# Moving the router's rows and the product for v on the Vector queue of an attention and MoE kernel

## The chip, the cores and the metric

One core of one Trainium2 chip runs the whole kernel in one launch. The metric is the device time of that launch in microseconds (us), lower is better; a run counts with its slowest core, which is the only one here. PE is the matrix engine (TensorE), DVE the vector engine, ACT the scalar engine, POOL is GpSimd and SP the engine that issues most of the DMAs.

## The reference, cut to what matters

One layer: attention with a layernorm in front of it and a residual, then a mixture of experts with the same. q, k and v come from the same normalised row by a phase and a table of sine and cosine; there are no projections.

```python
x = L0_attn_x                                   # 8 x 1024 x 512, f32
x = x + attn(layernorm(x))
x = x + ffn(layernorm(x))

def attn(x):                                    # 16 heads of 32
    theta_q = xh / (1 + abs(w_q)) + b_q + t * phi_q      # t: the position; k likewise
    Q = concat([cos(theta_q), sin(theta_q)]);  K = ...   # interpolated in a table
    theta_v = xh / (1 + abs(w_v)) + b_v;       V = cos_v + sin_v
    out = softmax(causal(Q @ K.T / sqrt(64))) @ V
    theta_o = out / (1 + abs(w_out)) + b_out
    return cos_o + sin_o

def ffn(x):                                     # 8 experts, 2 of them per token
    probs = softmax(x @ Wr + br)
    gate, expert = top_k(probs, 2)
    pos = place of the token among those of its expert, in order; kept if pos < 160
    y = (relu(rows of an expert @ W1 + b1)) @ W2 + b2
    return sum over the two of gate * y, where kept

def layernorm(x): return (x - mean) / sqrt(var + 1e-5)
```

## The kernel before, in words

**Two stages.** The attention runs as a loop over 32 chunks `n` (L1217): 8 sequences `b` of 1024 tokens by 4 chunks `c` of 128 features (4 heads). Then the experts run, expert by expert (`experts`, L1150). The last router works inside the first expert's time (`ending`, L1362); the other seven work inside the attention loop.

**What a chunk does.** `qk_pre(n)` (L477) turns the normalised rows on PE (transposes, L200, into a PSUM tile) and forms the phases of q and k with four DVE instructions (L493), which read that PSUM tile. `angle` (L423, its instruction L424) makes a second form of them on DVE; ACT computes squares, sines and cosines; `qk_post` (L523) multiplies on DVE and sends q and k to pairs of heads by DMA. `v_pre` (L543: L550, L555, L424) and `v_post` (L563, by `times`, L434) do the same for v without PE. `scores` (L599) multiplies q and k on PE (L608, the causal mask added at L622) and lets ACT take the exponential (L628). `attend` (L634) multiplies that by v on PE (L642) and copies the result out on DVE (L650). `turn` (L666), `o_pre` and `o_post` make the attention's output and its residual for the chunk before.

**PSUM.** `two_banks()` (L193) hands out tiles of a pool of three. Scores, the transposes of `qk_pre`, `turn` and the router, and the router's small products all take their tile from it, so each waits until an earlier user's reader is done.

**The router.** `router(b - 1)` (L695) is a generator that begins at the end of chunk 0 of sequence b (L1327) and is moved on by `next` or by `route_on(slot)`, which does so in chunk `slot` of a sequence. Its parts:
- Statistics, then `inverse_root` (L331), 1/sqrt by an integer guess and Newton steps of three DVE instructions each (L343 to L345). The first layernorm calls it too: 23 calls in all.
- `rows(t)` (L714) normalises 128 tokens on DVE (L716) into one of two buffers `xn2` and issues a store of them for the experts (L722, by SP). Rows 0 and 1 come with the first step.
- `features(g)` (L727), g from 0 to 3, transposes two such tiles on PE (L741) and copies them out on DVE (L743); then, up to g = 2, it makes the next two rows.
- `sums(g)` (L767) multiplies the features by the router's weights on PE (L779), copies the product `lg` (L784), and adds up the one before on PE and DVE (L762, L786).
- Softmax, choice of experts and places follow in chunks 2 and 3.

**What sets the order.** PE, DVE, ACT and SP run in the order in which the program issues its instructions (`manual_schedule`, L121). So an instruction's place in an engine's queue is its place in this program. Around chunk 1 of a sequence, where the router works, the order is, line by line:
- End of chunk 0: the router's statistics, roots and rows 0, 1 (L1327, L1328); v's product for the next chunk (L1344); part of the attention.
- Chunk 1: three steps of attention (L1254); features 0 and rows 2, 3 (L1255); `qk_pre(n + 1)` and `angle` (L1263, L1264); the load of a q/k base on SP (L1267); five scores with v's input between them (L1268); sums 0, then features 1 and rows 4, 5 (L1270, L1271); more attention; sums 1 (L1278); five scores; `turn`, `o_pre` (L1285); features 2 and rows 6, 7, with the store of the sequence's residual rows (L1287); attention; sums 2 (L1314); scores; `qk_pre(n + 2)` (L1330); features 3 (L1334); v's product (L1344); attention; sums 3 (L1346); five scores.

Of the kernel before, what the change touches and what calls it, by code (L numbers as in the profile page):

```python
# [25 lines left out]
NTT = S // P  # L26
# [47 lines left out]
def preln_attn_moe_kernel(  # L74
# [256 lines left out]
    def inverse_root(var, name):  # L331

        n = var.shape[1]
        v = small.tile([P, n], F32, name=f"{name}_v")
        y = small.tile([P, n], F32, name=name)
        t = small.tile([P, n], F32, name=f"{name}_t")
        nc.vector.tensor_scalar(v, var, EPS, None, ALU.add)
        nc.vector.tensor_scalar(
            y.bitcast(I32), v.bitcast(I32), -0.5, ROOT_GUESS, ALU.mult, ALU.add
        )  # L340
        nc.vector.tensor_scalar(v, v, -0.5, None, ALU.mult)
        for _ in range(4):
            nc.vector.tensor_tensor(t, y, y, ALU.mult)  # L343
            nc.vector.tensor_tensor(t, t, v, ALU.mult)
            nc.vector.scalar_tensor_tensor(y, t, 1.5, y, ALU.add, ALU.mult)  # L345
        return y
# [76 lines left out]
    def angle(p, r):  # L423
        nc.vector.tensor_scalar(r, p, TURN_SHIFT, None, ALU.logical_shift_left)  # L424
# [138 lines left out]
    def v_post(n, st):  # L563
        times(v_tiles[n % 2][:, :, :, :DH], heads(st[0]), heads(st[1].bitcast(F32)))


    def o_pre(n, pos):
        c = n % NCH
        p = pos.bitcast(I32)
        r = trig.tile([P, S], I32, name="t_r")  # L570
        nc.vector.tensor_tensor(by_token(p), by_token(pos), along(bias_o, c), ALU.add)
        angle(p, r)
        return p, r
# [86 lines left out]
    def rest(gen):  # L660
        got = None
        for got in gen:
            pass
        return got
# [30 lines left out]
    def router(b):  # L695
# [3 lines left out]
        def store():  # L699
            nc.sync.dma_start(token_tiles(out[b * S : (b + 1) * S, :]), xt)  # L700
# [13 lines left out]
        def rows(t):  # L714
            xn = row2.tile([P, D], F32, name="xn2")
            nc.vector.tensor_scalar(  # L716
                xn, xt[:, t, :], mv[:, t, 0:1], rstd[:, t : t + 1], ALU.subtract, ALU.mult
            )
            for d, (b0, b1_) in zip(xn2_d, REACH):
                if b0 <= b < b1_:  # L720
                    r0 = (b - b0) * S + t * P
                    nc.sync.dma_start(d[r0 : r0 + P, :], xn)  # L722
            return xn
# [3 lines left out]
        def features(g):  # L727

            xT = row2.tile([P, NCH, 2 * P], F32, name="xT", bufs=1)
            if last:  # L730
                for i, xn in enumerate(ahead):
                    ps = pools["ps_tr"].tile([P, NCH, P], F32, name="ps_t")
                    for c in range(NCH):
                        nc.tensor.transpose(ps[:, c, :], xn[:, c * P : (c + 1) * P], ident)
                    copy(xT[:, :, i * P : (i + 1) * P], ps)
            else:
                ps = two_banks()
                for i, xn in enumerate(ahead):
                    for c in range(NCH):
                        at = (NCH * i + c) * 64  # L740
                        by_halves(ps[:, :, at : at + 64], xn[:, c * P : (c + 1) * P])  # L741
                for a in range(2):
                    copy(  # L743
                        xT.rearrange("p c (i a q) -> p i c a q", a=2, q=64)[:, :, :, a, :],
                        ps[:, a, :].rearrange("p (i c q) -> p i c q", i=2, q=64),
                    )
            if g + 1 < NTT // 2:
                ahead[:] = [rows(2 * g + 2), rows(2 * g + 3)]
                if not last and 2 * g + 4 == NTT:
                    store()  # L750
            return xT

        def one_bank():
            if last:
# [39 lines left out]
        lg = None  # L794
        for g in range(NTT // 2):
            xT = features(g)
            yield
            lg = sums(g, xT, lg)
            yield
# [413 lines left out]
    last = None  # L1213
# [3 lines left out]
    for n in range(NCK):  # L1217
        more, late = n + 1 < NCK, last is not None
        b, c = divmod(n, NCH)
        if n == NCK - 1:  # L1220
            to_inputs.close()
            first_rows = experts_begin()
        pos_n = trig.tile([P, S], F32, name="o_p")
        if late:
            e11, halves1, pos = last
        es, halves = [[], []], [[], []]

        products = [attend(n, 0, h, es[h], halves[0]) for h in range(2)]  # L1230
        if late:
            products.insert(0, attend(n - 1, 1, 1, e11, halves1))
        ahead = [scores(pairs[0], h, es[h]) for h in range(2)]
        v_box = [None]
        asides = [keep(v_box, v_pre(n + 1))] if more else [first_rows]
        if b == 0 and c in (1, 2):
            asides.append(layernorm1(1, c - 1))
        elif c == 0 and b + 1 < B:
            asides.append(layernorm1(b + 1, 1))
        elif c == 3 and b + 2 < B:  # L1240
            asides.append(layernorm1(b + 2, 0))
        def route_on(slot):
            if c == slot and route is not None:
                next(route)

        def with_asides(count):
            for _ in range(count):
                some(1, *ahead)
                for g in asides:
                    next(g, None)  # L1250


        if late:
            some(3, *products)  # L1254
        route_on(1)  # L1255
        route_on(2)
        if c == 2 and route is not None:
            asides.append(part(route))
        if n == 0:
            with_asides(2)  # L1260
        if n == 0 or begin:

            qk_st = rest(qk_pre(n + 1))  # L1263
            angle(*qk_st)  # L1264
            angles = keep(place, both(qk_st))
            if begin:
                load_base(n + 2)  # L1267
        with_asides(3 if n == 0 else 5)  # L1268
        rest(residual)
        route_on(1)  # L1270
        route_on(1)  # L1271
        rest(angles)
        if more:
            v_st = v_box[0]
            square(v_st[0])
        if late:
            some(4, *products)
        route_on(1)  # L1278
        with_asides(5)
        for g in asides:  # L1280
            rest(g)
        if n == 1:
            load_mid(0)
        if late:
            turn(1, halves1, pos)  # L1285
            o_st = o_pre(n - 1, pos)
        route_on(1)  # L1287
        if n == 2:
            load_b1()
        if c == 3 and b > 0:  # L1290
            next(route)
            if b > 1:
                fetch_slots(b - 2)
            scatter()


        some(3, *products)
        if more:
            qk_st = place[0]
            qk_sin(qk_st)  # L1300
            sine(v_st[1])
        if late:
            sine(o_st[1])
        if more:
            post = qk_post(qk_st)
            next(post)
        some(NTT, *products)
        if n == 0:
            load_base(2)


        es, halves1 = [[], []], []
        ahead = [scores(pairs[1], h, es[h]) for h in range(2)]
        route_on(1)  # L1314
        route_on(2)
        some(2, *ahead)
        turn(0, halves[0], pos_n)
        next_pairs = rest(post) if more else None
        some(1, *ahead)
        if late:  # L1320
            square(o_st[0])
            residual = o_post(n - 1, o_st)
        some(2, *ahead)
        begin = c == 0 and late
        if begin:
            rest(residual)
            route = router(b - 1)  # L1327
            next(route)  # L1328
        elif n + 2 < NCK:
            qk_st = rest(qk_pre(n + 2))  # L1330

        if c != 1:
            next(residual, None)
        route_on(1)  # L1334
        if n + 2 < NCK and not begin and c != 1:
            angle(*qk_st)
        if c != 1:
            rest(residual)
        if c == 1 and b > 0:
            load_mid(b)  # L1340
        if c == 2 and b + 2 < B:
            load_x(b + 2)
        if more:
            v_post(n + 1, v_st)  # L1344
        some(3, attend(n, 1, 0, es[0], halves1))
        route_on(1)  # L1346
        if c == 1:

            angle(*qk_st)
        some(5, *ahead)  # L1350
        if n + 2 < NCK and not begin:
            angles = keep(place, both(qk_st))
            some(2, angles)
            if n + 3 < NCK:
                load_base(n + 3)
        last = (es[1], halves1, pos_n)
        pairs = next_pairs
# [55 lines left out]
```

## Time and profile before

| what | value |
|---|---|
| three runs | 3347.7, 3335.1, 3342.5 us; median 3342.5 |
| the profiled execution | 3335.3 us, its span 3333.5 us |
| PE busy | 3201.8 us (96%) |
| DVE busy | 2285.6 us (69%) |
| ACT busy | 1320.8 us (40%) |
| mean granted PE clock | 0.992 |

The attention loop takes the span up to about 1310 us, the experts the rest. A row of a timeline has start, duration (both us), engine, line, operation, the tile written, the tiles read, the shapes, and how many instructions of the kind were merged; a bracket at its end is idle time before it with what ended it. A row of the waits has the waiting engine, tile and line, what it waited for, then us in total, times, and the longest.

### The profile page before, as it was taken

The numbers are of one execution on the slowest core, as the hardware profiler recorded it, in microseconds if no ns is written. First come the engines' busy times: TensorE is split into PE (matmuls) and PEld (weight loads), VectorE is DVE, ScalarE is ACT, GpSimd is POOL, SyncE is SP. The second block draws the span as 40 slices with busy tenths as digits, with TensorE's granted clock in tenths as the row PEclk, the third lists the DMA queues.
The fourth block names the chain that finished last, engine by engine and source line by source line (L and its number), as shares of the span: only waits on it lengthen the run. The fifth ranks groups of instructions, "written<-read, shape, count | busy, mean of one in ns | idle before, by whom it ended". The sixth has DMA issues, their size and how long they took to land.

```text
span 3333.5 us, 48795 instructions
## 1 busy us (share of the span) xinstructions
PE 3201.8 (96%) x18942; PEld 2171.7 (65%) x18942; DVE 2285.6 (69%) x5064; ACT 1320.8 (40%) x1609; POOL 419.3 (13%) x363
## 2 busy tenths in 40 slices
PE   3999999999999999899999999999999999999998
PEld 1444444444444444588688688688688688688687
DVE  7887878788887675746746846845845845845854
ACT  5787888878787874201101101201201201201201
POOL 1000202020111103421011011011011011011010
PEclk9999999999999999999999999999999999999999
DMA  4445453545545343422312322322322422322321
GB/s 142 115 119 168 112 165 96 163 127 154 159 128 153 77 142 78 132 42 73 111 35 73 111 42 67 117 38 64 117 45 58 119 43 60 118 47 60 115 38 26
DMA packets 233966, 320.78 MB, mean 96 GB/s; under 512 B 21528, under 2 KB 154376, under 8 KB 221320
## 3 DMA queue, kind: packets, MB, share of 16 engines
q1 hardware_dynamic: 211120, 275.47, 27.8%
q0 software_dynamic: 22528, 42.18, 7.1%
q8 instruction: 150, 2.46, 0.3%
q14 instruction: 80, 0.66, 0.1%
q10 hardware_dynamic: 88, 0.02, 0.0%
HBM read 188.67 MB, written 61.82 MB: 75 GB/s over the span
## 4 chain that ended last, share of the span: by engine, by line
PE 57%; DVE 3%; DMA 1%; issue 1%; POOL 0%; ACT 0%; SPq 0%; POOLq 0%; DVEq 0%; ACTq 0%
PE ps_p L1084 29%; PE ps_p L1039 25%; PE ps_t L995 1%; PE av L642 1%; PE ps_s L608 1%; DMA slot_d<-token,slot 0%; DMA out_dram<-y,slots 0%; DVE t L1024 0%; DVE t L1023 0%; ACT hid L1071 0%; DVE hid L1067 0%; DMA xg<-xn_d,source 0%; DVE u L1065 0%; DVE hid L1068 0%; DVE hid L1069 0%
## 5 line engine op out<-in xcount | busy, mean ns | idle before, releaser
L628 ACT ACTIVATE e<-ps_s 128x1024 f32<-128x1024 f32 (+1 forms) x640 | 569.1, 938 | 225.0 <-PE ps_s L608 128.0
L608 PE MATMUL ps_s<-qk 64*128 64x512 f32 (+3 forms) x3072 | 599.4, 508 | 56.3 <-DMA qk<-qk_r 21.4
L1084 PE MATMUL ps_p<-w,hid 128*128 128x256 f32 x2560 | 570.6, 380 | 0.0
L1084 PEld LDWEIGHTS ps_p<-w,hid 128*128 128x128 f32 x2560 | 485.3, 191 | 66.7
L642 PE MATMUL av<-e,v 128*64 128x512 f32 (+3 forms) x3072 | 523.9, 490 | 0.0
L1084 PE MATMUL ps_p<-w_t,hid 128*128 128x256 f32 x1920 | 430.0, 379 | 0.0
L608 PEld LDWEIGHTS ps_s<-qk 64*128 64x128 f32 x3072 | 263.8, 189 | 240.8 <-issue 140.6
L1084 PEld LDWEIGHTS ps_p<-w_t,hid 128*128 128x128 f32 x1920 | 361.9, 190 | 47.7
L642 PEld LDWEIGHTS av<-e,v 128*64 128x64 f32 x3072 | 200.6, 137 | 283.5 <-issue 268.0
L1039 PE MATMUL ps_p<-xe_s,t 128*128 128x256 f32 (+1 forms) x1024 | 299.4, 435 | 5.5 <-DVE t L1024 3.4
L1039 PE MATMUL ps_p<-xe,w 128*128 128x256 f32 (+1 forms) x1024 | 302.4, 439 | 1.2 <-issue 1.1
L1039 PE MATMUL ps_p<-xe,t 128*128 128x256 f32 (+1 forms) x1024 | 296.9, 433 | 0.0
L690 POOL DMA_INDIRECT slot_d<-token,slot x128 | 163.9, 1281 | 1013.1 <-issue 431.6
L1113 ACT COPY p<-ps_p 128x256 f32<-128x256 f32 x40 | 14.8, 369 | 614.0 <-PE ps_p L1084 614.0
L1039 PEld LDWEIGHTS ps_p<-xe_s,t 128*128 128x128 f32 x1024 | 194.2, 191 | 90.5 <-DVE t L1024 7.9
L1039 PEld LDWEIGHTS ps_p<-xe,w 128*128 128x128 f32 x1024 | 194.6, 192 | 85.2 <-DVE hid L1057 5.8
L1039 PEld LDWEIGHTS ps_p<-xe,t 128*128 128x128 f32 x1024 | 194.6, 190 | 81.3 <-issue 1.0
L978 POOL DMA_INDIRECT xg<-xn_d,source x80 | 78.3, 979 | 1104.3 <-PE ps_t L995 1024.4
L1106 POOL DMA_INDIRECT out_dram<-y,slots x80 | 126.5, 1581 | 664.2 <-DVE y L1101 528.7
L1054 ACT ACTIVATE p<-ps_p,b_t 128x256 f32<-128x256 f32 (+1 forms) x128 | 65.5, 512 | 330.7 <-DVE y L1100 169.7
L1058 ACT ACTIVATE hid<-hid 128x256 f32<-128x256 f32 (+1 forms) x128 | 60.1, 470 | 322.3 <-DVE hid L1057 322.3
L1071 ACT ACTIVATE hid<-hid,b_more 128x256 f32<-128x256 f32 (+1 forms) x128 | 71.8, 561 | 271.2 <-DVE hid L1070 271.2
(210 smaller groups left out, 3840.9 us busy)
## 6 DMA issues: line engine op xcount, KB each, us to landing
w<-in_L_ffn_W_dram SPq DMA_DIRECT2D x256, 256.0 KB
qk<-qk_c SPq DMA_DIRECT2D x128, 256.0 KB
qk<-qk_r SPq DMA_DIRECT2D x128, 256.0 KB
w<-in_L_ffn_W_dram SPq DMA_DIRECT2D x64, 512.0 KB
qk_base<-base_d SPq DMA_DIRECT2D x29, 1024.0 KB
xn_d<-xn SPq DMA_DIRECT2D x72, 256.0 KB
x_mid<-in_L_attn_x_dram SPq DMA_DIRECT2D x16, 1024.0 KB
out_dram<-x_mid SPq DMA_DIRECT2D x8, 2048.0 KB
```

The source lines that it names most:

```text
L608: nc.tensor.matmul(ps[:, a, at : at + w], lhsT=pair[r, 1, kb * P : (kb + 1) * P], rhs=pair[r, 0, q0 : q0 + w], start=at == 0, stop=not own ...
L628: nc.scalar.activation(e, ps[:, :, :n], AF.Exp, scale=UNIT * UNIT / math.sqrt(2 * DH))
L642: nc.tensor.matmul(av[a * 64 : (a + 1) * 64, q0 - 512 * h :], lhsT=vt[:, kb, 2 * pr + a, :], rhs=es[i][:, a, at : at + w], start=kb == 0, ...
L690: nc.gpsimd.indirect_dma_start(out=slot_d[b], out_offset=bass.IndirectOffsetOnAxis(ap=idx, axis=0), in_=src, in_offset=None,)
L978: nc.gpsimd.indirect_dma_start(out=xg, out_offset=None, in_=xn2_d[i % 2], in_offset=bass.IndirectOffsetOnAxis(ap=source[:, e, j0 + j, None ...
L995: nc.tensor.transpose(ps[:, c, :], xg[:, c * P : (c + 1) * P], ident)
L1039: nc.tensor.matmul(ps, lhsT=weights[:, k, :], rhs=rows[:, k, :], start=k == 0, stop=k == 1)
L1054: nc.scalar.activation(p1, product(b11, a11), AF.Identity, bias=b1_t[:, e * NHC + q : e * NHC + q + 1])
L1058: nc.scalar.activation(h11, h11, AF.Relu)
L1071: nc.scalar.activation(h12, h12, AF.Relu, bias=more)
L1084: nc.tensor.matmul(ps, lhsT=hs[k][:, part, cols], rhs=ws[k][weight], start=k == 0, stop=k == NHQ - 1,)
L1106: nc.gpsimd.indirect_dma_start(out=out, out_offset=bass.IndirectOffsetOnAxis(ap=meta[:, e, jj[r], 0:1], axis=0), in_=ys[r], in_offset=None ...
```

## The change

Five edits:
- `inverse_root` makes three Newton steps in place of four.
- The next rows are no longer a part of `features`. In the seven routers of the loop they are a step of their own after it; in the last router they still come straight after it.
- In chunk 1, v's product (which stood at the end of chunk 0) and the step with rows 2 and 3 come after `qk_pre(n + 1)` and ahead of `angle` and the base's load.
- Features 3 come ahead of `qk_pre(n + 2)`, not behind it.
- The calls of `route_on` are counted anew, so that rows 4, 5 follow features 1 and rows 6, 7 follow features 2 as before.

```diff
-        for _ in range(4):
+        for _ in range(3):
             nc.vector.tensor_tensor(t, y, y, ALU.mult)
             nc.vector.tensor_tensor(t, t, v, ALU.mult)
             nc.vector.scalar_tensor_tensor(y, t, 1.5, y, ALU.add, ALU.mult)
...
-            if g + 1 < NTT // 2:
-                ahead[:] = [rows(2 * g + 2), rows(2 * g + 3)]
-                if not last and 2 * g + 4 == NTT:
-                    store()
             return xT
+
+        def next_rows(g):
+            ahead[:] = [rows(2 * g + 2), rows(2 * g + 3)]
+            if not last and 2 * g + 4 == NTT:
+                store()
...
             xT = features(g)
+            if g + 1 < NTT // 2:
+                if not last:
+                    yield
+                next_rows(g)
             yield
             lg = sums(g, xT, lg)
             yield
...
             qk_st = rest(qk_pre(n + 1))
+            if begin:
+                v_post(n, v_st)
+                next(route)
             angle(*qk_st)
             angles = keep(place, both(qk_st))
...
         rest(residual)
-        route_on(1)
-        route_on(1)
+        for _ in range(3):
+            route_on(1)
         rest(angles)
...
             o_st = o_pre(n - 1, pos)
+        route_on(1)
         route_on(1)
...
         elif n + 2 < NCK:
+            route_on(1)
             qk_st = rest(qk_pre(n + 2))
 
         if c != 1:
             next(residual, None)
-        route_on(1)
...
-        if more:
+        if more and not begin:
             v_post(n + 1, v_st)
```

## The prediction

> **What bounds the kernel now.** I read the page first, for who is busy, then the list of waits with PE as the waiting engine, then the timelines of DVE and PE around one router.
>
> ```profile
> PE 3201.8 (96%) x18942; PEld 2171.7 (65%) x18942; DVE 2285.6 (69%) x5064; ACT 1320.8 (40%) x1609; POOL 419.3 (13%) x363
> ```
>
> PE is busy for 96% of the span, so an edit on another engine gains only where PE waits for it. The list of waits (total us, times, longest) says where that is:
>
> ```profile
> PE ps_s L608 <- DVE qk_f L493: 13.7, 7, 3.1
> ...
> PE ps_s L608 <- DVE xT L743: 7.9, 7, 1.1
> PE ps_s L779 <- DVE xT L743: 6.6, 8, 0.8
> ```
>
> Nearly all lie in the seven routers of the attention loop (the first row once at the start too, 0.2 us; router 5 has the third twice and not the first): scores (L608) wait until DVE has read a PSUM tile out, either the router's transposed rows (L743) or the inputs of q and k (L493); the router's last product (L779) waits for its features. Together 28.2 us, the most that these waits can give. What stands in front of them on DVE, third router:
>
> ```profile
> 559.55 1.00 DVE L716 TENSOR_SCALAR xn<-x_mid,mv,rstd 128x512 f32<-128x512 f32 x2
> 560.47 1.24 DVE L434 SCALAR_TENSOR_TENSOR v<-v_p,t_r 128x1024 f32<-128x1024 f32 x1
> 561.63 0.74 DVE L650 TENSOR_SCALAR av_sb<-av,inv_o 128x512 f32<-128x512 f32 x1
> 562.29 1.27 DVE L743 COPY xT<-ps_s 128x512 f32<-128x512 f32 x2
> 563.49 1.03 DVE L716 TENSOR_SCALAR xn<-x_mid,mv,rstd 128x512 f32<-128x512 f32 x2
> 564.44 2.71 DVE L493 SCALAR_TENSOR_TENSOR qk_f<-ps_s,inv_qk,qk_base 128x512 int32<-128x512 f32 x4
> 567.18 1.23 DVE L424 TENSOR_SCALAR qk_r<-qk_f 128x2048 int32<-128x2048 int32 x1
> 568.32 1.29 DVE L550 TENSOR_TENSOR v_p<-xn,inv_v 128x512 f32<-128x512 f32 x2
> ...
> 571.51 0.42 DVE L784 COPY lg<-ps_s 128x256 f32<-128x256 f32 x1
> 571.85 1.28 DVE L743 COPY xT<-ps_s 128x512 f32<-128x512 f32 x2
> ```
>
> No row has idle time before it: for 20 us DVE is a full queue. PE beside it (brackets: idle before, and what ended it):
>
> ```profile
> 560.35 1.21 PE L200 MATMUL ps_s<-ident,xn 64*128 64x64 f32 x32
> ...
> 563.71 1.14 PE L608 MATMUL ps_s<-qk 64*128 64x384 f32 x8 [1.15 <-DVE xT L743]
> ...
> 567.20 1.99 PE L608 MATMUL ps_s<-qk 64*128 64x512 f32 x8 [1.67 <-DVE qk_f L493]
> ...
> 573.63 0.62 PE L779 MATMUL ps_s<-xT,wr_sb 128*32 128x256 f32 x8
> ...
> 598.69 0.64 PE L779 MATMUL ps_s<-xT,wr_sb 128*32 128x256 f32 x8 [0.83 <-DVE xT L743]
> ```
>
> I call the router's transposes F0 to F3, its row pairs R0 (rows 2, 3) to R2, its products S0 to S3. F0 and q/k's transposes are at 560.35, S1 at 573.63, S3 at 598.69. The DVE list of waits has one more row that matters:
>
> ```profile
> DVE xn L716 <- DMA xn_d<-xn: 4.4, 4, 1.4
> ```
>
> In four routers R0 also waits for the store that frees its row buffer, with q/k's inputs queued behind it.
>
> [...]q/k's four readers run in program order behind R0, though their data is there at 561.6. [...]after waits of 2.93 and 2.45 us (routers 2 and 4) the clock granted over 411.6 to 415.0 and 722.0 to 725.4 was 0.52 and 0.55, but 3.15 us in router 6 did nothing. [...]
>
> **The change, part by part.**
>
> *Three Newton steps.* Three instructions every 0.20 us: 0.6 less on DVE per call, 23 calls. At the start DVE runs without a gap from the roots to the first q and k, and PE waits for these: 0.6 gained. In the last router PE waits 2.4 us for its first rows: 0.6 gained. In the seven loop routers it only brings R(0, 1) forward, whose reader F0 is on PE's time: nothing by itself. Fourteen calls in the first layernorm lie where no PE wait follows: nothing. Sum 1.2 (0 to 2).
>
> *R0 and v's product behind the inputs of q and k.* They stood for 0.95 (563.49 to 564.44) and 1.16 us (560.47 to 561.63), start to start. Without them xT's copies start when F0 is done, 0.75 after its first transpose (the gap that DVE shows after the second transposes, 415.68 to 416.44), so 561.10 for 562.29; q/k's inputs then end at 565.0 for 567.15. The first wait of PE goes (its score needs the bank at 562.56, xT is out at 562.3); the second shrinks to about 0.7. PE would come to S1 2.8 us sooner, 10.46 after F0 (13.28 less 1.15 and 1.67).
>
> But S1 needs lg and xT, and on DVE these lie behind everything moved. Nothing but Newton's steps left the queue, and in place of these DVE now idles for F0. Start to start, from F0's first transpose: 0.75, xT 1.20, q/k 2.74, v 1.16, R0 0.95, angle 1.14, v's inputs 3.19, lg 0.34, xT 1.28, and 0.05 to PE: 12.80 us. That is later than PE's 10.46, so S1 comes 12.80 after F0, with a new wait of PE of some 1.6 us there beside the 0.7. Before, this distance was 13.24, 16.17, 13.28, 15.69, 14.35, 14.74 and 13.33 (timelines of the seven routers): 100.8 in sum, now 89.6. **11.2 us**, of which 9.8 come from the four routers with a late store or a halved clock: R0 now comes 6 us after the rows whose stores it waits for (they took up to 4.9, 871.0 to 875.9 in router 5), so that wait ends[...].
>
> What queues behind the moved work: v's product has its first reader, the new chunk's attention, at 580.0, 13 us later. R0's stores stay ahead of the q/k base's load on SP, 2.6 us later; that base is read near 595. F1 on PE needs R0 at 567.5, and it is out at 567.1. R1 reuses R0's buffers at 573.0; at 4.9 us a store lands at 572.0: a margin of 1 us. v's product and F issue no DMA, and nothing is moved past POOL's work.
>
> *R1, R2 as steps of their own.* They follow F1 and F2 as before: nothing. ACT gets its scores sooner, so the 0.16 that F2 waits for an exponential in each of the seven goes: **1.1**.
>
> *F3 ahead of q/k's inputs.* The 0.83 at S3 goes in seven routers, 5.8 us. But q/k's inputs now end at 598.6 for 597.4, and lg and prob of S3, which free S3's bank, stay at 600.84, since DVE has the same work in between. Three tiles rotate: of the three scores behind S3, starting at 598.43, the third needs at 600.33 either S3's bank or that of the first, whose exponential ends near 600.7. About 0.5 comes back, 0.33 stays: **2.3** (0 to 5.8).
>
> Sum: 1.2 + 11.2 + 1.1 + 2.3 = **15.8 us**. Against the profiled execution, 3335.3 (span 3333.5), that is 3319.5. The median of the three runs, 3342.5, lies 7.2 above it; I carry the difference over: **3326.7**. A slower run may hold more late stores and halved clocks, which the change would remove too, so the error is rather upwards in gain.
>
> **Rivals.**
>
> *Everything goes.* If DVE keeps up with PE at S1 (some step of the 12.80 overlaps), all waits named go: 7 x 10.46 for 100.8 is 27.6, with 5.8, 1.1 and 1.2 gives 35.7: 3306.8. For it: the rows' ends overlap the next starts by 0.1. Against: the sum is of starts, which has that in it. Chance 0.18.
>
> *A new wait for a store.* R1 waits for R0's stores, which now share the queues with the 1 MB load of the q/k base. If they take 1.3 us over the margin, lg of S1 and the third score's bank are late by as much: 7 x 1.3 = 9 back, 3336 (between 3330 and 3341 for 0.5 to 2 us). For it: four such waits before. Against: the stores are issued ahead of that load. Chance 0.24.
>
> *Slower: banks.* Which of three PSUM tiles a score takes is settled when the program is built. If the first score behind S1 and S3 gets the bank that lg and prob still hold, it waits 1.5 at S1 (575.1 for 573.6) and 2.4 at S3 in place of 0.5: 3.4 x 7 = 24 lost, 3351. It decides from 15.8/7 = 2.3 us a router. For it: in router 5 the scores take other banks than in the rest (there S0 waits for q/k's inputs, not a score). Against: in all seven, the score behind S1 never waits. Chance 0.06.
>
> **How the numbers follow.** The forecast has 0.52; its own range is 3320 to 3332 (2 us on the S1 sum, S3 from 0 to 5.8, Newton from 0 to 2). The range 3311 to 3339 reaches from most of the first rival to the second and leaves out its far side and the banks. A half of one per cent, about what a measurement of this kernel can tell from no change, is 16.7 us: the line is at 3325.8, just under the forecast. Faster: the first rival and 0.32 of the forecast, 0.50. Same: the other 0.20 and the second rival, 0.44. Slower 0.06.
>
> **What would show it.** L716's wait for xn_d gone; scores no longer waiting for L743; L493's wait near 0.7 a router; a new wait of L762 and L779 at S1 for lg and xT, about 1.6 together; S1 at 12.8 after F0 in all seven; no wait at S3, but one of about 0.5 at the third score behind it; DVE's count down by 69. I am wrong if S1 comes near 10.5 after F0, or if L716 waits again at R1.

## The result, and the profile after

| | kernel before | changed kernel |
|---|---|---|
| median, us (10 runs each) | 3343.7 | 3329.9 |
| lowest and highest run | 3335.1, 3347.7 | 3325.6, 3332.7 |
| profiled execution, and its span | 3335.3, 3333.5 | 3331.3, 3329.4 |

The ratio is 0.996, 95% interval 0.9952 to 0.9968: some 13.4 us faster, 10.7 to 16. The forecast was 3326.7 in 3311 to 3339, a gain of 15.8. So the time is in the range, and the gain a little smaller than forecast. It is less than the half per cent (16.7 us) at which the prediction divided its chances: 0.50 had been given to a larger gain, 0.44 to one like this. A second measurement of the same two kernels (told below) gave 0.9969 (0.9957 to 0.9981).

The two profiled executions alone lie only 4.1 us apart. That pair misleads, and one of the experiments shows why.

The changed file is a few lines longer: what was L779, L784, L786 and L1039 is now L780, L785, L787 and L1044. First, as before, the page's row of the engines and the list of PE's waits (us in total, times, longest), changed kernel:

```profile
PE 3200.2 (96%) x18942; PEld 2170.5 (65%) x18942; DVE 2269.0 (68%) x4992; ACT 1321.1 (40%) x1609; POOL 417.2 (13%) x363
```

```profile
PE ps_p L1044 <- POOL t L1029: 10.3, 2, 6.7
...
PE ps_s L780 <- DVE xT L743: 5.5, 7, 0.8
PE ps_s L608 <- DVE qk_f L493: 4.1, 8, 0.6
PE ps_s L608 <- DVE prob L787: 4.0, 7, 0.6
...
PE ps_s L763 <- DVE lg L785: 3.5, 7, 0.6
...
PE ps_s L200 <- ACT e L628: 1.1, 7, 0.2
```

DVE runs 72 instructions fewer, not 69: `inverse_root` is called 24 times and not 23 (its L343 ran 96 times in the kernel before, four to a call).

The scores' wait for L743 is gone, and 13.7 us for L493 have become 4.1. In their place stand two waits, seven times each: L763 for lg, which the kernel before had once (0.4 us), and L608 for prob, which it did not have. The row for xT has nearly the same total as before, but it is another wait: it was the one at S3, and is now the one at S1. DVE's list of waits has no row in the loop any more in which L716 waits for the store of xn_d.

The third router on DVE, in the changed kernel:

```profile
555.31 1.00 DVE L716 TENSOR_SCALAR xn<-x_mid,mv,rstd 128x512 f32<-128x512 f32 x2
556.23 0.74 DVE L650 TENSOR_SCALAR av_sb<-av,inv_o 128x512 f32<-128x512 f32 x1
557.46 1.29 DVE L743 COPY xT<-ps_s 128x512 f32<-128x512 f32 x2 [0.49 <-PE ps_s L200]
558.67 2.72 DVE L493 SCALAR_TENSOR_TENSOR qk_f<-ps_s,inv_qk,qk_base 128x512 int32<-128x512 f32 x4
561.30 1.21 DVE L434 SCALAR_TENSOR_TENSOR v<-v_p,t_r 128x1024 f32<-128x1024 f32 x1
562.43 0.99 DVE L716 TENSOR_SCALAR xn<-x_mid,mv,rstd 128x512 f32<-128x512 f32 x2
563.35 1.22 DVE L424 TENSOR_SCALAR qk_r<-qk_f 128x2048 int32<-128x2048 int32 x1
...
567.67 0.42 DVE L785 COPY lg<-ps_s 128x256 f32<-128x256 f32 x1
568.00 1.28 DVE L743 COPY xT<-ps_s 128x512 f32<-128x512 f32 x2
```

and on PE:

```profile
556.71 1.21 PE L200 MATMUL ps_s<-ident,xn 64*128 64x64 f32 x32
...
561.44 1.99 PE L608 MATMUL ps_s<-qk 64*128 64x512 f32 x8 [0.55 <-DVE qk_f L493]
...
568.23 0.31 PE L763 MATMUL ps_s<-gather_e,lg 128*32 128x8 f32 x16 [0.43 <-DVE lg L785]
569.33 0.64 PE L780 MATMUL ps_s<-xT,wr_sb 128*32 128x256 f32 x8 [0.79 <-DVE xT L743]
...
593.42 0.62 PE L780 MATMUL ps_s<-xT,wr_sb 128*32 128x256 f32 x8
...
596.53 1.13 PE L608 MATMUL ps_s<-qk 64*128 64x512 f32 x4 [0.58 <-DVE prob L787]
```

DVE now idles 0.49 ahead of the first copies, as there is nothing left to do while F0 runs; from there to the second copies it is a full queue again. PE meets it first at the inputs of q and k (0.55), then at S1, at 569.33, 12.62 after F0's first transpose. S3, at 593.42, waits for nothing; the third score behind it waits 0.58.

The distance from F0 to S1 in all seven routers, from the timelines of PE. In the kernel before, a store was late in routers 2, 4, 5 and 6 (L716 waited four times, 4.4 us in all), and behind it the granted clock was 0.52 in router 2 (411.6 to 415.0) and 0.55 in router 4 (722.0 to 725.4):

| F0 to S1, us | 1 | 2 | 3 | 4 | 5 | 6 | 7 | sum |
|---|---|---|---|---|---|---|---|---|
| before | 13.24 | 16.17 | 13.28 | 15.69 | 14.35 | 14.74 | 13.33 | 100.8 |
| before, second profile | 13.23 | 16.52 | 13.27 | 16.22 | 15.03 | 14.16 | 13.39 | 101.8 |
| changed | 12.63 | 12.77 | 12.62 | 12.77 | 12.78 | 12.64 | 12.63 | 88.8 |

The distance before varies from one execution to the next, with the stores that happen to be late. In the five profiles of kernels in which the rows and v's product were not moved (two of the kernel before, three from the experiments below) the sum lies between 96.3 and 102.5, and L716 waits for a store in three or four routers. In the five profiles in which they were moved and v's inputs left where they were (two of the changed kernel, three from below) the sum lies between 88.8 and 89.9, and L716 waits for no store in the loop. The means are 10.7 apart.

S1 to S3 went from 25.06 (25.09 in router 5) to 24.09; S3 to the next F0 rose from 115.7 to 116.5 in most.

### The profile page after: what moved, and what is told of

Its sections match the earlier page's. It is cut to its first block, busy times and chain, and to the rows that moved or that the text cites. A ratio compares the mean times of both kernels' runs of the same rounds, so it can differ in the third digit from the quotient of the medians.

```text
span 3329.4 us, 48736 instructions
## 1 busy us (share of the span) xinstructions
PE 3200.2 (96%) x18942; PEld 2170.5 (65%) x18942; DVE 2269.0 (68%) x4992; ACT 1321.1 (40%) x1609; POOL 417.2 (13%) x363
## 4 chain that ended last, share of the span: by engine, by line
PE 84%; DVE 7%; DMA 3%; issue 2%; ACT 2%; POOL 1%; SPq 0%; POOLq 0%; DVEq 0%; ACTq 0%
PE ps_p L1089 29%; PE ps_p L1044 27%; PE av L642 13%; PE ps_s L608 12%; DMA slot_d<-token,slot 2%; ACT e L628 2%; PE ps_s L200 1%; PE ps_t L1000 1%; PE ps_s L622 1%; DVE qk_f L493 1%; DVE qk_r L434 1%; DVE v L434 0%; DVE xT L743 0%; SPq L533 0%; DVE v_p L550 0%
## 5 line engine op out<-in xcount | busy, mean ns | idle before, releaser
L608 PE MATMUL ps_s<-qk 64*128 64x512 f32 (+3 forms) x3072 | 596.5, 505 | 42.6 <-DMA qk<-qk_r 21.4
L608 PEld LDWEIGHTS ps_s<-qk 64*128 64x128 f32 x3072 | 262.4, 188 | 228.1 <-issue 128.2
L1044 PE MATMUL ps_p<-xe_s,t 128*128 128x256 f32 (+1 forms) x1024 | 301.7, 438 | 13.7 <-POOL t L1029 10.3
L1044 PE MATMUL ps_p<-xe,w 128*128 128x256 f32 (+1 forms) x1024 | 299.7, 436 | 1.2 <-issue 1.1
L1044 PE MATMUL ps_p<-xe,t 128*128 128x256 f32 (+1 forms) x1024 | 297.1, 433 | 0.0
L1044 PEld LDWEIGHTS ps_p<-xe_s,t 128*128 128x128 f32 x1024 | 195.2, 192 | 99.3 <-POOL t L1029 11.4
L1044 PEld LDWEIGHTS ps_p<-xe,w 128*128 128x128 f32 x1024 | 193.6, 191 | 83.4 <-DVE hid L1062 4.8
L1044 PEld LDWEIGHTS ps_p<-xe,t 128*128 128x128 f32 x1024 | 194.7, 190 | 81.4 <-issue 1.3
```

The lines of the kernel that those rows point to most:

```text
L608: nc.tensor.matmul(ps[:, a, at : at + w], lhsT=pair[r, 1, kb * P : (kb + 1) * P], rhs=pair[r, 0, q0 : q0 + w], start=at == 0, stop=not own ...
L1044: nc.tensor.matmul(ps, lhsT=weights[:, k, :], rhs=rows[:, k, :], start=k == 0, stop=k == 1)
```

## The experiments

The theory was the prediction's: behind F0 the work on DVE is one queue, S1 comes when its part in front of lg and xT is done, and moving q's and k's inputs to its front gains only until this queue, and no longer PE, sets S1. The main rival was that the single edits are worth what the waits in front of them show, and add. Each kernel below was timed against the kernel before on the same chip. Kernels of one group share these runs: 3338.35 us in the first (35 runs), 3338.38 in the second (20), 3342.85 in the third (10). "Less than before" is taken from the ratio on record, which is not the quotient of the two medians; the two differ by up to 3 us. The changed kernel itself was timed again in the third group alone.

### Each part alone

Three Newton steps alone:

```diff
-        for _ in range(4):
+        for _ in range(3):
```

> The kernel before with three Newton steps and nothing else. Theory (the DVE queue sets S1): DVE is 0.6 us early at every one of the seven routers and both waits of the scores are for that queue, so the distance from F0 to S1 shrinks by about 0.6 in each (13.24 to about 12.65 where no store is late); with 0.6 at the start and 0.6 in the last router some 5 us, 3338 to 3340. Rival, as the prediction has it: in the loop the steps only bring rows forward whose reader is on PE's time, so 1.2 us, 3342 to 3343, and F0 to S1 unchanged.

3337.1 us, ratio 0.9994 (0.9984 to 1.0004): between 5.3 us less and 1.3 more. So no gain is shown, and the time rules out neither the prediction's 1.2 us nor the 5 of my new theory. The trace speaks against the new theory. F0 to S1 was 12.62, 16.25, 13.16, 17.45, 14.06, 15.77 and 13.17, in sum 102.5: not less than before. Where no store had been late the distance fell by 0.62, 0.12 and 0.16. In the same four routers as before L716 waited for its stores, now seven times and 5.3 us in place of four times and 4.4:

```profile
DVE xn L716 <- DMA xn_d<-xn: 5.3, 7, 1.1
```

Rows 2 and 3 came to their buffers sooner, and the buffers were not free sooner.

Rows 2, 3 and v's product alone, with four Newton steps and features 3 behind q and k as before:

```diff
-        for _ in range(3):
+        for _ in range(4):
             nc.vector.tensor_tensor(t, y, y, ALU.mult)
...
         elif n + 2 < NCK:
-            route_on(1)
             qk_st = rest(qk_pre(n + 2))
...
             next(residual, None)
+        route_on(1)
```

> The changed kernel with four Newton steps and features 3 behind the inputs of q and k, as before: only rows 2, 3 and the product for v are moved. Theory: F0 to S1 12.6 to 12.9 in all seven routers, no wait of L716 for a store, no halved clock in the loop; 10 to 12 us less than before, about 3332. S3 waits 0.83 for its features as before. Rival (the moved work itself gains little, Newton's steps and features 3 the rest): less than 6 us.

3328.3 us, ratio 0.9966 (0.9954 to 0.9978): 11.3 us less. F0 to S1 was between 12.63 and 13.30, two of the seven (12.99 and 13.30) above what I expected, with no wait of L716 for a store. The mean granted clock was 0.994 over the whole of the profiled execution, 0.992 in that of the kernel before; the clock in the loop alone is not shown. So this edit is the change; the rest adds little to it. It also shows where the gain of an undisturbed router comes from: with four Newton steps, routers 1, 3 and 7 came to 12.63, 12.70 and 12.74, so the 0.6 gained there does not need the shorter roots. In these routers S1 waited for nothing before, and PE's own path set it (13.24 to 13.33); now the queue does. Over all seven routers the sum is 89.9 here and 88.8 with three steps. The rows and v's product were moved together in every run; which of the two matters more is not shown.

Features 3 alone:

```diff
         elif n + 2 < NCK:
+            route_on(1)
             qk_st = rest(qk_pre(n + 2))
...
             next(residual, None)
-        route_on(1)
```

> The kernel before with features 3 ahead of the inputs of q and k and nothing else. Theory: S1 to S3 25.06 becomes 24.1, and the third score behind S3 waits 0.6 for prob, so 0.2 to 0.4 us a router, 1.5 to 3 in all: 3341 to 3342. Rival: nothing is given back, 0.97 a router, 6.8 us: 3337.

3334.7 us, ratio 0.9990 (0.9983 to 0.9997): 1.0 to 5.7 us less. S1 to S3 fell from 25.06 to 24.07 (24.09 in router 5), and the third score waited 0.58 for prob in each of the seven routers, as expected. The interval holds the 1.5 to 3 us that I expected and leaves out the rival's 6.8. The profile does not show what is kept: over the six stretches from S3 to the next F0 it is 7.8 us longer than the kernel before, more than S1 to S3 gave, and its F0 to S1 is 96.3 in sum, 4.5 less, though nothing in front of S1 had been edited.

### Is S1 set by the queue?

v's inputs (3.19 us of DVE) and the square that follows are taken out from between q's and k's angle and lg, and put behind S1, where DVE idled for 3.7 us. Nothing in front of F0 changes.

```diff
-        with_asides(3 if n == 0 else 5)
+        if begin:
+            for _ in range(5):
+                some(1, *ahead)
+        else:
+            with_asides(3 if n == 0 else 5)
...
-        if more:
+        if more and not begin:
             v_st = v_box[0]
             square(v_st[0])
...
         for g in asides:
             rest(g)
+        if begin:
+            v_st = v_box[0]
+            square(v_st[0])
```

> The changed kernel with v's inputs (3.19 us of DVE) and v's square put behind the product S1 in the seven router chunks, into DVE's idle time of 3.7 us ahead of the turn. Theory (the DVE queue in front of lg and xT sets S1): these leave the queue, S1 comes as soon as PE is there, 10.9 to 11.2 us after F0 where the changed kernel has 12.62 to 12.78, no wait for lg or xT; 7 x 1.6 = 11 us less than the changed kernel, 3318 to 3321. Rival: S1 is set by something else, or the time comes back in the turn or at the exponentials behind it: less than 3 us, above 3327.

3318.0 us, ratio 0.9931 (0.9918 to 0.9945): 23 us less than before where the changed kernel has 13.4. In the profiles, S3 of the seventh router comes 9.2 us sooner than in the changed kernel (1197.43 and 1206.58). In this kernel's third router, on DVE:

```profile
560.08 1.22 DVE L424 TENSOR_SCALAR qk_r<-qk_f 128x2048 int32<-128x2048 int32 x1
561.21 0.41 DVE L785 COPY lg<-ps_s 128x256 f32<-128x256 f32 x1
561.55 1.27 DVE L743 COPY xT<-ps_s 128x512 f32<-128x512 f32 x2
...
565.63 0.16 DVE L787 TENSOR_TENSOR prob<-ps_s,br_b 128x16 f32<-128x16 f32 x1
565.72 1.28 DVE L550 TENSOR_TENSOR v_p<-xn,inv_v 128x512 f32<-128x512 f32 x2
567.03 1.23 DVE L555 TENSOR_TENSOR v_p<-v_p,bias_v 128x1024 int32<-128x1024 f32 x1
568.29 0.69 DVE L424 TENSOR_SCALAR t_r<-v_p 128x1024 int32<-128x1024 int32 x1
570.23 0.26 DVE L677 RECIPROCAL rec<-ps_s 128x16 f32<-128x16 f32 x1 [1.25 <-PE ps_s L200]
```

and on PE:

```profile
553.23 1.21 PE L200 MATMUL ps_s<-ident,xn 64*128 64x64 f32 x32
...
564.46 0.31 PE L763 MATMUL ps_s<-gather_e,lg 128*32 128x8 f32 x16
564.61 0.62 PE L780 MATMUL ps_s<-xT,wr_sb 128*32 128x256 f32 x8
```

lg comes straight after the angle, and both waits at S1 are gone. F0 to S1 is 11.17 in four routers and 11.32 to 11.60 in the others. The moved work fits where DVE was idle, with 1.25 of that left. This is the experiment that decides: with not one instruction fewer on DVE, and none moved in front of F0, S1 comes 1.4 us sooner on the mean (12.69 to 11.28). The queue set it. What is left is close to PE's own path: the 10.46 of the prediction, and the wait for the inputs of q and k, 0.55 to 0.72 here. v's square, which runs on ACT, was moved too; that the square played no part is argued from the waits at S1, both of which were for DVE, and not from a run of its own.

It also shows the second rival of the prediction at work. L716 waits again for xn_d, now for rows 4 and 5 in five of the routers, 5.0 us in the loop: in the third router row 4 comes 3.57 us behind row 2 (559.17 to 562.74) where the changed kernel has 6.77. DVE has time there, so PE hardly notices: S1 to S2 is 14.42, and 14.53 in router 5, which has the longest of these waits, 1.9.

### Where features 3 gave the time back

v's product of the router chunk, which stands in front of lg and prob of S3 on DVE, is put behind them.

```diff
-        if more and not begin:
+        if more and not begin and (c != 1 or route is None):
             v_post(n + 1, v_st)
         some(3, attend(n, 1, 0, es[0], halves1))
         route_on(1)
+        if c == 1 and route is not None:
+            v_post(n + 1, v_st)
```

> The changed kernel with v's product of the router chunk put behind the router's product S3, its lg and its prob. Theory (features 3 in front gave the time back to the bank that lg and prob of S3 hold): 1.16 us of DVE leave the queue in front of prob, so the third score behind S3 no longer waits, S3 to the next F0 is 0.8 shorter in each of the seven routers; 5 to 6 us less than the changed kernel, about 0.9945 of the kernel before. Rival: the third score then waits for the first score's exponential instead, or v's product is late for its reader: less than 2 us.

3321.7 us, ratio 0.9954 (0.9941 to 0.9967), 15.3 us less than before. Against the changed kernel's 0.996 and 0.9969 that is 2 to 5 us, a little under the 5 to 6 expected; the intervals overlap, so the times alone don't settle it. The trace does. PE behind S3 of the third router:

```profile
591.36 0.62 PE L780 MATMUL ps_s<-xT,wr_sb 128*32 128x256 f32 x8
591.91 2.85 PE L608 MATMUL ps_s<-qk 64*128 64x512 f32 x12
```

The three scores run as one row with no bracket, and prob's row is gone from the list of PE's waits. Over the six stretches from S3 to the next F0 the sum fell from 700.3 to 695.9 us (694.5 in the kernel before): 4.4 in six, about what the third score had lost.

Both moves at once:

> Both moves: v's inputs behind S1 and v's product behind S3. Theory: the two queues are apart by 14 us in which DVE idles, so the gains add: 10 us and 5 to 6 us less than the changed kernel, about 0.9915 of the kernel before, 3311 where that is 3340. Rival: one takes up what the other gave, and it is within 3 us of the kernel with v's inputs alone (0.993).

3313.0 us, ratio 0.9916 (0.9903 to 0.993): 28 us less than before. The interval overlaps that of v's inputs alone, so again the times don't settle it. In the profiles they add: S3 of the seventh router comes 13.6 us sooner than in the changed kernel (1192.99), where v's inputs alone gave 9.2 and v's product alone 4.7 (1201.84).

### What happens to the gain between the loop and the experts

The loop hands over to the first expert at its first product (L1039, now L1044). The next landmark is the first transpose of the second half's rows (L995, now L1000), which waits for a gather. Between the two the first profiles differ much: 134.7 us before, 142.2 in the changed kernel, and the list of PE's waits blames POOL: 10.3 us against 2.1. POOL mixes the first expert's weights, and its queue holds the 16 scatters of router 7. I took it that a loop that ends sooner is held up there.

```diff
-        mix = nc.gpsimd.tensor_tensor if i == 0 else TT
+        mix = nc.gpsimd.tensor_tensor if i == 0 and q < 2 else TT
```

> The changed kernel with the mixing of the first chunk's weights, from the third slice on, on DVE and not on POOL, where it queues behind the 16 scatters of the seventh and eighth router. Theory (POOL's queue takes back a part of what the loop gained): the two waits of PE for POOL in the first expert, 10.3 us, go; DVE gets 1.7 us a slice more, so some comes back: 3 to 8 us less than the changed kernel. Rival: DVE is the bound there already, and the time is the same or longer.

3320.1 us, ratio 0.9944 (0.9931 to 0.9957): 18.7 us less than before, 5 to 8 less than the changed kernel by its two ratios.

> The same edit on the kernel before. Theory: its waits for POOL there are shorter (2.1 us in the profiled execution), so it gains less than the changed kernel does, and the two kernels with this edit lie further apart than 13.7 us, by up to 4. Rival (POOL's queue costs both the same): both gain or lose alike, and the distance stays 13 to 14 us.

3330.8 us, ratio 0.9978 (0.9970 to 0.9986): 7.4 us less than before. So the edit gives the kernel before about as much; with it the medians lie 10.7 us apart. That is no further apart than without it, against my theory, though the intervals leave some 5 us either way. From first product to gather both now take 130.3, where the kernels without the edit, in all their profiles, take 134.7 to 142.8. So the rival fits better: POOL's queue costs both kernels alike. Then the first profile of before would be the odd one:

> The kernel before once more, unaltered, for a second profile. Theory (the first profiled execution was a lucky one between the loop and the experts, not typical): from the first expert's first product to the first gather of its second half 136 to 140 us, where the first profile has 134.7. Rival (only kernels that come early to the experts are held up there): 134 to 135 again.

3345.0 us in its profiled execution, span 3343.2; from first product to gather 142.8.

```profile
PE ps_p L1039 <- POOL t L1024: 8.0, 2, 4.6
```

8.0 us for POOL in place of 2.1. 142.8 is above the 136 to 140 of the theory, and further still from the rival. The first profiled execution (3335.3) was as quick as the fastest of its kernel's ten runs (3335.1), and of the 9.7 us between the two spans 8.1 lie in this stretch. In the first, POOL came from the scatters to the mixing 27.0 us after the first product; in this one 33.9 us after it, in the two profiles of the changed kernel 33.7 and 34.0. Why the scatters went quicker that once is not shown.

> The changed kernel once more, unaltered, for a comparison on the chip of the kernels beside it. Both theories: 0.995 to 0.997 of the kernel before, and from the first expert's first product to the first gather of its second half 138 to 143 us, as in the other kernels that reach that point early.

3331.4 us, ratio 0.9969 (0.9957 to 0.9981). F0 to S1 is 12.63 or 12.78 in all seven, and first product to gather 140.0. The spans of this profile and of the one just before, both from this group, lie 17.1 us apart, the first pair 4.1, and the medians 11.4 here and 13.7 in the first measurement: pairs of single profiles say little about a change of this size.

### The three moves together

> The changed kernel with v's inputs behind S1, v's product behind S3, and the first expert's later mixing on DVE. Theory: the three stand at different places and add: 0.9916 less 0.002, 0.989 to 0.990 of the kernel before, the quickest of all. Rival: the loop's earlier end is lost again at the experts' start: 0.9915 or above.

3303.7 us, ratio 0.9884 (0.9869 to 0.9899): 39 us less than the kernel before, 28 less than the changed one on the same chip. F0 to S1 is 11.17 in all seven. First product to gather is 128.4.

## Why the prediction was right, and where it was off

By its own steps. Up to S3 of the seventh router the first two profiled executions lie 13.65 us apart (1220.23 and 1206.58).

**The queue in front of S1**, forecast 11.2: right. 12.80 after F0 was said, 12.62 to 12.78 came, and the sum fell by 12.0. The new waits were said to be 0.7 and some 1.6; they show as 0.55 and 1.2 to 1.4. Most of the 12.0 comes from the routers in which a store had been late (10.0 of it in routers 2, 4, 5 and 6: 3.40 + 2.92 + 1.57 + 2.10), as forecast. In routers 2 and 4 the fall holds the clock too, 0.52 and 0.55 before and 1.00 over 119.0 to 1261.9 us in the changed kernel; what ties the clock to the wait is not shown, and that part of the forecast was the author's estimate. How much the fall is depends on the execution: by the means of five profiles each the fall is 10.7. Taking v's inputs out of the queue moved S1; that was the test of it.

**Newton's steps**, forecast 0.6 at the start, 0.6 in the last router, nothing in the loop. In the second router of the kernel before, the three instructions of a step took 0.16 to 0.17 us each and started 0.20 apart (400.26, 400.46 and 400.66, the next step at 400.86). The start gave 0.64 in the first two profiles (F0 of the first router 249.48, then 248.84); over all profiles it lies at 248.6 to 251.0 with four steps and at 248.2 to 249.1 with three, so a single pair does not prove it. In the last router PE's wait for its first rows fell from 2.4 to 1.7, but the waits for POOL behind it differ by far more from one execution to the next, so whether 0.6 is kept to the end is not shown. Alone, the steps gave 2 us, with no change inside the interval. That agrees with 1.2; it is F0 to S1 in the trace, and not the time, that speaks against the 5 that I expected of that experiment.

**F2's wait for an exponential**, forecast 1.1: wrong. The row stands unchanged, 1.1 us, 7 times. The failing step was "ACT gets its scores sooner, so the 0.16 ... goes". It took ACT to be behind. Before, ACT's five exponentials did follow on v's square without a gap, and in the changed kernel ACT idles 1.42 us ahead of them; but they start 1.79 us after S1 before (575.42) and 1.81 after it now (571.14), so there was no backlog to win back. F2 waits for an exponential of these scores, which come as long after S1 as before. S1 to S2 is 14.42 before and 14.44 after.

**Features 3**, forecast 2.3: the mechanism was right, the size off. The gain, S1 to S3, was 0.97 a router (0.83 forecast). What comes back at the third score shows as 0.58 (0.5 forecast) but costs 0.8: from S3's product to the mask behind that score PE took 3.25 us before (598.69 to 601.94) and 4.05 after (593.42 to 597.47). So the term that was mis-sized is what comes back: 0.8 where 0.5 was reckoned. A shown wait of 0.83 gave 0.97 when it went, and one of 0.58 cost 0.80 when it came: 0.14 and 0.22 more than the brackets say. Net that is 0.17 a router, some 1 us in all.

So 15.8 becomes 13.65 at S3 of the seventh router: 0.64 at the start, 12.0 at S1, and 6.8 at S3 less 5.8 in the six stretches behind it. Of these 5.8, 4.8 are the third scores, and most of the rest is one stretch with a wait of 1.1 for an exponential. That this is so near the medians' 13.4 to 13.7 is partly luck. The seventh third score comes behind this point, and at the first expert's first product the profiles lie 10.8 us apart (13.8 in the second pair, which has 16.6 at S3); where the other 2 us go was not followed up.

**The rivals.** "Everything goes" fails at S1: PE waits there for lg and xT in every router. A new wait for a store did not come in the changed kernel, where rows 4, 5 start 6.8 us behind rows 2, 3, and does come when they start sooner, at almost no cost. The banks: in all kernels run, the first score behind S1 and S3 never waited for prob; where a score did, it was the third behind S3, as forecast.

**The step to the median.** I carried over the 7.2 us between the profiled execution and the median, and said that the difference might hide more of the same stalls. In the second profile it did not: the sum of F0 to S1 is within 1 us of the first (101.8 and 100.8), and most of the difference is POOL's stretch at the start of the experts. So carrying the 7.2 us over was right, for a reason that the prediction did not have.

## What to carry to other kernels

When work is moved back in a full queue, ask which consumer stands behind its new place. Here the gain ended where the queue up to that consumer became the later of the two engines' paths (S1 at 12.6 for 13.3 in a router without a late store), and the next gain came from moving work past that consumer into the engine's next idle stretch (S1 at 11.17 to 11.60). Sum the queue from its first release to the consumer, start to start, and compare it with the other engine's own path: here the sums were 12.80 and 10.46, and 12.62 to 12.78 came. Take a second profile of the baseline before two single executions are subtracted from each other.

## What the runs showed that I had not expected

- Work that came sooner only waited longer for a buffer: with three Newton steps alone L716 came sooner and waited for the stores 5.3 us in place of 4.4, in the same four routers, and F0 to S1 did not shrink in sum.
- Two executions of the same kernel differ by 8 us in one stretch (134.7 and 142.8 us from the first product of the experts to the second half's rows), with the loop ahead of it the same within 2.6 us.
- In routers 2 and 4 of the kernel before the granted clock was about half, 0.52 over 411.6 to 415.0 us and 0.55 over 722.0 to 725.4, and the score behind the wait took 3.63 and 3.43 us where it took 1.99 in router 6. In the second profile of that kernel it took 3.18 and 3.65 in routers 2 and 4. The granted clock of the changed kernel was 1.00 over 119.0 to 1261.9 us of its span, which is from ahead of the first router to past the seventh. In the first profile the longest wait did not go with a lower clock: PE waited 2.93 and 2.45 us in routers 2 and 4 and 3.15 in router 6, where the clock was 1.00 over 1030 to 1038.
